# A hand-written order of the last ten tiles is replaced, the last tile's sums go to two PSUM banks, and one copy of queries moves ahead of a transpose

## The chip, the cores and the metric

The kernel runs on one core of one Trainium2 chip. The metric is device time in microseconds of one execution. The engines are TensorE (PE; its weight loads are listed apart as PEld), VectorE (DVE), ScalarE (ACT), GpSimd (POOL) and SyncE (SP), which only issues transfers here. Each engine works through its own instructions in the order in which the program gives them; between engines there are semaphores. PE writes to PSUM, which has eight banks of 128 partitions by 512 fp32 numbers.

## The reference

Cross-attention with a residual and a layer norm. `x` has 4 batches of 2048 rows of 512, the context 4 times 77 rows, and there are 16 heads of 32:

```python
qs = (q @ wq).reshape(Bq, Lq, H, HD).transpose(0, 2, 1, 3)
ks_ = (k @ wk).reshape(Bq, Lk, H, HD).transpose(0, 2, 1, 3)
vs = (v @ wv).reshape(Bq, Lk, H, HD).transpose(0, 2, 1, 3)
scores = jnp.einsum('bhqd,bhkd->bhqk', qs, ks_) / jnp.sqrt(jnp.float32(HD))
scores = jnp.where(mask[:, None, :, :], -jnp.inf, scores)
attn_w = jax.nn.softmax(scores, axis=-1)
attn = jnp.einsum('bhqk,bhkd->bhqd', attn_w, vs)
attn = attn.transpose(0, 2, 1, 3).reshape(Bq, Lq, H * HD)
out = attn @ wo + q
mu = jnp.mean(out, axis=-1, keepdims=True)
var = jnp.mean((out - mu) ** 2, axis=-1, keepdims=True)
return (out - mu) / jnp.sqrt(var + EPS) * gamma + beta
```

Here `q` is `x` and `k` and `v` are the context.

## The kernel before

The 8192 rows are 64 tiles of 128 rows. Tiles t = 2b and 2b + 1 make pair b; four tiles make a group, whose queries come from one block of transposed `x`. Products in full precision are made of three fp32r matmuls each (a number is split into a high and a low part). The first three pairs are written out in a loop of their own; pairs 3 to 26 run the list of words `PAIR`; what is left of the last pairs and tiles 54 to 63 is the list `JOINT` and then `ORDER`, which `do()` carries out word by word. The words set the order in which each engine gets its instructions, and nothing else does. A word is a letter, a tile (or pair, or query block) and a part; in `PAIR` the number is relative to the pair.

- `S54` scores of tile 54 (PE, L321), four banks, one for each fourth of the heads. `T54.1` the maxima of one fourth, 4 heads (DVE, L364), which reads the second of these banks and adds the mask. `e54.1` the exponentials (ACT, L379), `r54` the reciprocals of the sums (DVE, L385), `n54` the normalising product (POOL, L390), `t54` a transpose in blocks of 32 (DVE, L413).
- `P26.7g` the seventh of twelve transfers that regroup the transposed pair 26 into `PT` (L425); the last letter names the queue that issues it: s is SP, a is ACT, g is POOL. `U62.7s` is the same for tile 62 alone. `V26` then multiplies pair 26 with the values (PE, L459; two banks, half of the heads to each), `a26.0` and `b26.0` split the first half's result into high (ACT, L508) and low (DVE, L512).
- `O54` the output projection of tile 54 (PE, L557; one bank, 12 matmuls), `x54` loads its rows, `+54` adds them (DVE, L560).
- `Q59` queries of block 59, that is a fourth of the columns for one group (PE, L192; one bank), `q59` copies them out (DVE, L209). `i31` and `j31` split half a group of transposed `x` (ACT, POOL).
- Layer norm: `s` mean and variance on DVE (L595, L601), or `I` and `J` the same on ACT (L615, L621); `u` the reciprocal root on POOL (L631, L632); then either `y` and `z` on DVE (L655, L664), or `v`, `k` and `f` on POOL, ACT and POOL (`p` is `v` and `k` in one on POOL, L645), or `y`, `K` and `G` on DVE, ACT and POOL. `w` stores the tile.
- Tile 63 has a way of its own: `h`, `m`, `R` and `E` turn it with PE, `W` multiplies one tile with the values (L492, L474), `c` and `d` split it, `X63` adds its rows by matmuls with the identity (L540), and `O63` goes by halves of the columns. `finish_last` stores by halves, on SP and ACT.
- `M0` and `M1` keep the rows gamma and beta in a PSUM bank from there on, which leaves the ring one bank fewer.

`bank()` (L107) deals the eight banks in turn: a tile gets the buffer of the eighth grant before it, and its first matmul waits until that buffer's last reader is through. The order of the grants is that of the words.

The words on PE in `ORDER` run: S54 O49 S55 Q59 O48 S56 V25 S57 Q62 Q60 Q63 S58 Q61 V26 S59 O51 O50 S60 V27 S61 O52 O53 O54 S62 V28 O55 O57 S63 V29 O56 O59 O58 V30 R63.0 R63.1 R63.3 R63.2 O60 O61 X63 W62 W63 O62 O63.

For tile 54 the word `y54` (which subtracts the mean in place and multiplies by gamma) stands ahead of `J54` (which sums the squares about the mean).

## Time and profile before

| | us |
|---|---|
| three runs | 507.15, 506.95, 507.97; median 507.15 |
| the profiled execution | 506.96 |
| its span, first to last instruction | 505.2 |
| outside its span | 1.76 |
| PE, granted clock over the span | 0.998 |
| ORDER on PE, first to last matmul | 413.48 to about 498.6 |

The profile's times count from the first instruction. The page gives the busy time of each engine, the chain of waits that ended last, and groups of equal instructions; the trace behind it gives rows in order of time (start, length, engine, line, operation, tiles), busy times by stretch, and a list of who waited for whom. A row's length can overlap the next one's on the same engine, so what an instruction costs in a full queue is the distance from its start to the next start.

### The profile page before, as it was taken

Reading aid. Unit: us, or ns where it says so; the run is one execution under the profiler, and the core shown is the slowest. Engines: PE = TensorE matmul, PEld = TensorE weight load, DVE = VectorE, ACT = ScalarE, POOL = GpSimd, SP = SyncE. Lnnn points to the kernel's source line nnn. Section 1 sums busy time; section 2 is a strip of 40 time slices with the busy share of each in tenths; the row PEclk is TensorE's granted clock in tenths of the full one; section 3 lists DMA queues with packets and bytes.
Section 4 is the critical chain, followed back from the end, with each engine's and each line's share of the span. In section 5 each row is a group of like instructions: output and inputs, shape, how many; then the busy total and the mean of one; then the engine's idle time right before and its main releaser. Section 6 shows DMA issues by size and latency. Waiting matters only on the chain.

```text
span 505.2 us, 20438 instructions
## 1 busy us (share of the span) xinstructions
PE 496.4 (98%) x6908; PEld 391.0 (77%) x6908; DVE 463.3 (92%) x2566; ACT 472.2 (93%) x2239; POOL 427.0 (85%) x384
## 2 busy tenths in 40 slices
PE   9999999999999999999999999999999999999994
PEld 7987778777777887777788777777877777777784
DVE  6698999999989998999999988999999889999997
ACT  6798999999999999999999999999999999999861
POOL 0659368989888998988999888889988888999994
PEclk9999999999999999999999999999999999999999
DMA  8945887677778779777878878787777878667665
GB/s 308 399 165 151 207 215 194 197 191 210 213 226 227 217 211 257 188 205 227 224 218 220 237 182 248 210 228 212 228 200 204 237 214 245 171 189 209 168 210 209
DMA packets 58280, 109.50 MB, mean 217 GB/s; under 512 B 9203, under 2 KB 10739, under 8 KB 58176
## 3 DMA queue, kind: packets, MB, share of 16 engines
q1 hardware_dynamic: 55776, 103.35, 72.5%
q0 software_dynamic: 1872, 4.20, 2.7%
q8 instruction: 55, 0.90, 0.8%
q10 hardware_dynamic: 528, 0.66, 0.4%
q14 instruction: 49, 0.40, 0.2%
HBM read 41.68 MB, written 16.78 MB: 116 GB/s over the span
## 4 chain that ended last, share of the span: by engine, by line
PE 90%; ACT 4%; DVE 3%; DMA 2%; issue 1%; SPq 1%; DVEq 0%; ACTq 0%
PE pq L192 31%; PE po L557 29%; PE pa L459 11%; PE sc L321 7%; PE sc L557 3%; ACT pbuf L379 3%; PE sc_e L321 2%; PE pv L258 2%; PE pk L218 1%; PE pq L709 1%; PE pq L190 1%; DMA PT<-B 1%; PE sc_f L321 1%; DMA xtf<-xT 1%; DVE pbuf L364 1%
## 5 line engine op out<-in xcount | busy, mean ns | idle before, releaser
L379 ACT ACTIVATE pbuf<-pbuf,nm 128x77 f32<-128x77 f32 x1024 | 352.5, 349 | 8.5 <-DVE nm L364 7.5
L379 ACT ACTIVATION_READ_ACCUMULATOR pbuf<-pbuf,nm 128x1 f32 x1024 | 193.5, 189 | 0.0
L390 POOL TENSOR_TENSOR pbuf<-pbuf,ri 128x1232 f32<-128x1232 f32 x63 | 145.9, 2317 | 19.7 <-DVE ri L385 15.7
L364 DVE CUSTOM_DVE_ANT_0 pbuf<-sc,mb 128x77 f32<-128x77 f32 x828 | 144.0, 232 | 5.9 <-PE sc L321 5.6
L192 PE MATMUL pq<-xtl,wqh 128*128 128x512 f32 (+1 forms) x256 | 98.3, 384 | 0.0
L192 PE MATMUL pq<-xth,wql 128*128 128x512 f32 (+1 forms) x256 | 98.2, 384 | 0.0
L413 DVE STREAM_TRANSPOSE B<-pbuf 128x1280 f32<-128x1280 f32 x63 | 94.6, 1503 | 0.4 <-POOL pbuf L390 0.2
L557 PE MATMUL po<-woh,AH 128*128 128x512 f32 x224 | 90.6, 405 | 0.0
L192 PE MATMUL pq<-xth,wqh 128*128 128x512 f32 (+1 forms) x230 | 88.6, 385 | 0.0
L557 PE MATMUL po<-wol,AH 128*128 128x512 f32 x224 | 87.4, 390 | 0.0
L585 POOL TENSOR_TENSOR o<-o,gam 128x512 f32<-128x512 f32 x53 | 68.7, 1297 | 21.0 <-ACT o L581 21.0
L557 PE MATMUL po<-woh,AL 128*128 128x512 f32 x224 | 86.5, 390 | 0.0
L364 DVE DVE_READ_ACCUMULATOR2_ANT nm<- 128x1 f32 x1024 | 84.7, 83 | 0.0
L586 POOL TENSOR_TENSOR o<-o,bet 128x512 f32<-128x512 f32 x53 | 68.4, 1290 | 4.2
L180 POOL TENSOR_TENSOR xtl<-xtf,xth 128x1024 fp32r<-128x1024 f32 x28 | 67.5, 2412 | 0.1
L459 PE MATMUL pa<-PT,vsb 96*32 96x256 f32 x960 | 58.2, 382 | 0.7 <-DMA PT<-B 0.3
L321 PE MATMUL sc<-kct,q 32*64 32x77 f32 x3312 | 55.2, 238 | 0.5 <-DVE q L209 0.5
L192 PEld LDWEIGHTS pq<-xth,wql 128*128 128x128 f32 x256 | 48.2, 188 | 8.4
L192 PEld LDWEIGHTS pq<-xtl,wqh 128*128 128x128 f32 x256 | 48.1, 188 | 8.5
L321 PEld LDWEIGHTS sc<-kct,q 32*64 32x64 f32 x3312 | 48.7, 130 | 6.5 <-issue 4.8
L557 PEld LDWEIGHTS po<-woh,AH 128*128 128x128 f32 x224 | 42.0, 188 | 10.8 <-DVE nm L364 0.4
L192 PEld LDWEIGHTS pq<-xth,wqh 128*128 128x128 f32 x230 | 43.2, 188 | 9.0
(176 smaller groups left out, 851.6 us busy)
## 6 DMA issues: line engine op xcount, KB each, us to landing
PT<-B SPq DMA_DIRECT2D x355, 128.0 KB
xtf<-xT SPq DMA_DIRECT2D x28, 512.0 KB
o<-x SPq DMA_DIRECT2D x56, 256.0 KB
out<-o SPq DMA_DIRECT2D x56, 256.0 KB
PT<-B POOLq DMA_DIRECT2D x16, 128.0 KB, 4.5
o_end<-x SPq DMA_DIRECT2D x7, 256.0 KB
out<-o_end SPq DMA_DIRECT2D x7, 256.0 KB
xtf<-xT SPq DMA_DIRECT2D x4, 256.0 KB
```

The source lines that it names most:

```text
L180: nc.gpsimd.tensor_tensor(l, fx.pop((g, c)), h.bitcast(F32), ALU.subtract)
L192: nc.tensor.matmul(pq, wc, r[:, c, rs], start=(n == 0), stop=(n == 11))
L258: nc.tensor.matmul(pv, ctx_s[c][i][:, r, :], v[c], start=(n == 0), stop=(n == 11))
L321: nc.tensor.matmul(scs[t][g, j][r0 : r0 + n], qd[t // 4][q, g, at : at + n], kct[q, g, t // TPB, keys_of(j)], start=True, stop=True,)
L364: nc.vector.tensor_tensor_reduce(pb[:, i // 2, (i % 2) * NK : (i % 2 + 1) * NK], scs[t][g, j], mb[:, t % TPB, keys_of(h)], -1.0, CEIL, ALU ...
L379: nc.scalar.activation(p, p, AF.Exp, bias=nmax[t][:, i : i + 1], scale=-1.0, accum_out=sums[t][:, i : i + 1])
L390: nc.gpsimd.tensor_tensor(pv, pv, rv.to_broadcast((P, NP, 2, NK)), ALU.mult)
L413: nc.vector.transpose(bt.rearrange("p c q r -> p q c r"), pbuf[t % NPB].rearrange("p q (c r) -> p q c r", c=5),)
L459: nc.tensor.matmul(pas[b, g // 2][HD * j : HD * (j + 1), (g % 2) * BLK : (g % 2 + 1) * BLK], vsb[:, 2 * b // TPB, HD * h : HD * (h + 1)], ...
L557: nc.tensor.matmul(pos[t][:, cols], a[:, c, rs], w[:, c, cols], start=go, stop=done)
L585: nc.gpsimd.tensor_tensor(o, o, gam, ALU.mult)
L586: nc.gpsimd.tensor_tensor(o, o, bet, ALU.add)
```

## The change

- `JOINT` and `ORDER` are replaced by one new list. Nearly all words are the same ones in another order. Gone are I54 and J54, s58, s60, s62, v56, k56, f56 and p50; new are s54 (ahead of y54), I58, J58, I60, J60, I62, J62, y56, K56, G56, v50 and k50. The transfers change queues: on POOL's there are 15 for 16, on ACT's 5 for 3, the rest is on SP's.
- The words on PE now run: S54 Q59 S55 S56 O48 O49 S57 V25 Q63 S58 Q62 Q61 Q60 S59 V26 S60 O51 O50 S61 V27 O52 O53 S62 V28 O54 O55 O57 S63 V29 O56 O58 O59 V30 R63.1 R63.0 O61 R63.3 R63.2 O60 W62 W63 O62 X63 O63.
- The words on DVE now begin: q58 b24.0 T54.1 T54.0 T54.3 T54.2 b24.1 q59 T55.2 T55.3 T55.0 t53 T56.2 T56.1 r54 T56.3 +48 T55.1 T56.0 s48 t54 T57.3; around tile 59 they run q60 T59.0 q62 T59.2 T59.1 T59.3 t57, around tile 62 t59 T62.2 b27.0 +52 T62.1; and they end with z61 z58 +62 d63 y60 z60 y62 s63 z62 y63 z63.
- M0 comes later, and M1 is the last word but one, behind z63, so that beta is read from SBUF.
- Tile 63's projection has a PSUM bank for each half of the columns, and `X63`, the statistics and `y63` go by these halves.
- In pair 3 the word q6 (the copy of query block 12) is put ahead of t0; before, that copy was the first DVE work of pair 4's q4.

```diff
-JOINT = """ a24.1 b24.0 b24.1 """
-
 ORDER = """
-S54 T54.3 i31 e54.3 T54.0 O49 q58 e54.0 k47 T54.2 T54.1 +49 t53 S55 T55.0 T55.1 Q59 f47 x50 x52 T55.3 e54.2 T55.2
-e54.1 j31 r54 n54 O48 q59 s49 P26.9s +48 S56 e55.0 P26.4s e55.2 e55.1 e55.3 T56.1 T56.0 P26.6g P26.0s V25 T56.2 x51
...
+q58 i31 b24.0 S54 T54.1 k47 Q59 T54.0 a24.1 T54.3 e54.1 T54.2 b24.1 e54.2 S55 q59 j31 S56 T55.2 e54.0 T55.3 T55.0 O48
+e54.3 t53 f47 x61 e55.0 T56.2 P26.3s T56.1 P26.5s e55.2 r54 T56.3 n54 P26.0s +48 w47 e55.3 T55.1 O49 x58 T56.0 S57
+P26.11s P26.6g e55.1 s48 V25 x50 t54 u48 x52 e56.1 x51 P26.1g T57.3 x59 Q63 P26.4g e56.3 r55 P26.9s T57.0 n55 T57.2
+P26.2s e56.0 T57.1 P26.8s +49 P26.10s S58 p48 e56.2 t55 x53 Q62 a25.0 T58.0 P27.9s e57.3 P26.7g r56 b25.0 x57 n56
+T58.3 P27.2s a25.1 Q61 s49 e57.2 P27.10s b25.1 P27.5s T58.2 P27.0g e57.0 x56 q63 P27.1g x55 Q60 f48 q61 e57.1 P27.4s
+t56 P27.6s k46 P27.11s T58.1 e58.3 P27.7s r57 S59 q60 n57 P27.3s T59.0 e58.1 P27.8s q62 V26 T59.2 e58.2 f46 T59.1 S60
+T59.3 a26.1 O51 t57 a26.0 e58.0 T60.1 P28.8s P28.5g T60.0 e59.3 P28.9g w46 O50 T60.2 u49 P28.6s T60.3 e59.1 P28.10g
+P28.1s r58 +51 P28.3g P28.2s b26.0 n58 e59.0 b26.1 S61 x54 +50 e59.2 V27 P28.4s s51 P28.11s s50 u51 e60.0 P28.7s r59
+t58 O52 n59 a27.1 e60.1 T61.0 T61.2 P28.0g e61.2 T61.1 O53 p49 b27.1 T61.3 a27.0 e61.3 t59 u50 S62 e61.1 v51 T62.2
+P29.10s P29.7g b27.0 V28 P29.5s f49 e61.0 +52 x62 T62.1 P29.3s O54 a28.0 +53 a28.1 P29.6s r61 s52 e60.3 n61 P29.1s s53
...
+O63 w58 I62 y60 w61 J62 z60 y62 w60 u62 s63 w59 z62 u63 y63 w62 z63 M1 w63
@@ resid
-        pos[t] = bank(f"po_{t}")
-        if t < NT - 4:
-            nc.tensor.matmul(pos[t], ident, od[t], start=True, stop=False)
-            return
+        pos[t] = [bank(f"po_{t}")[:, cols] for cols in HALVES]
         place(t)
...
-                nc.tensor.matmul(pos[t][:, c * P : (c + 1) * P], rows_t, unit, start=(c == 0 and n == 0), stop=False)
+                po = pos[t][c // 2][:, c % 2 * P : (c % 2 + 1) * P]
+                nc.tensor.matmul(po, rows_t, unit, start=(c % 2 == 0 and n == 0), stop=False)
@@ o_proj
-        halves = [slice(0, D)] if t < NT - 1 else HALVES
-        for cols in halves:
+        for po, cols in [(pos[t], slice(0, D))] if first else zip(pos[t], HALVES):
             for n, (_, c, a, w) in enumerate(prods):
...
-                nc.tensor.matmul(pos[t][:, cols], a[:, c, rs], w[:, c, cols], start=go, stop=done)
+                nc.tensor.matmul(po, a[:, c, rs], w[:, c, cols], start=(first and n == 0), stop=(n == 11))
@@ moments_one
-            for n, cols in enumerate(HALVES):
-                nc.vector.bn_stats(st[:, n], pos.get(t, od[t])[:, cols])
+            for n, po in enumerate(pos[t]):
+                nc.vector.bn_stats(st[:, n], po)
@@ centre
+        for po, cols in zip(pos[t], HALVES):
+            nc.vector.scalar_tensor_tensor(od[t][:, cols], po, mean, gam[:, cols], ALU.subtract, ALU.mult)
@@ pair
             words.insert(words.index("D"), "O-6")
+            words.insert(words.index("t0"), "q6")
```

More of the change, by code (lines that the diff above doesn't have):

```diff
@@ L51 @@
 """
-JOINT = """ a24.1 b24.0 b24.1 """
 ORDER = """
-S54 T54.3 i31 e54.3 T54.0 O49 q58 e54.0 k47 T54.2 T54.1 +49 t53 S55 T55.0 T55.1 Q59 f47 x50 x52 T55.3 e54.2 T55.2
-e54.1 j31 r54 n54 O48 q59 s49 P26.9s +48 S56 e55.0 P26.4s e55.2 e55.1 e55.3 T56.1 T56.0 P26.6g P26.0s V25 T56.2 x51
-r55 a25.0 a25.1 t54 e56.1 S57 e56.2 T56.3 T57.2 Q62 P26.2g P26.8s n55 e56.3 T57.1 Q60 t55 u49 b25.0 e56.0 P26.3g Q63
-e57.1 p49 e57.2 T57.3 T57.0 r56 w47 s48 b25.1 P26.5s x59 e57.3 x53 S58 P26.10s P26.7g P27.7g q62 e57.0 k46 n56 q60
@@ L59 @@
-P27.0s q63 u48 p48 T58.1 T58.2 P26.1s P27.1s P26.11s T58.3 e58.1 r57 t56 P27.11s n57 Q61 P27.6s f46 e58.2 T58.0 V26
-q61 a26.1 t57 a26.0 x55 f48 e58.0 S59 P27.2s T59.2 P27.5s e58.3 T59.3 e59.3 P27.3s P28.4g P27.8s T59.0 O51 b26.0
-P28.11g T59.1 P27.9s +51 P28.6g r58 e59.2 P28.5g O50 P27.10s b26.1 s51 e59.1 P27.4s n58 S60 Y0 u51 +50 P28.0s x57
-e59.0 P28.7g P28.10s V27 T60.0 T60.1 a27.0 T60.2 a27.1 T60.3 e60.1 r59 t58 w46 P28.3s P28.9s S61 n59 O52 P28.1s
-e60.3 b27.0 s50 T61.0 T61.3 t59 f49 u50 e61.0 e61.3 T61.2 b27.1 T61.1 O53 P28.8s P29.1g P29.9g e61.2 O54 S62 +52
@@ L64 @@
-e61.1 +53 s52 x54 r61 P28.2s V28 +54 P29.7g e60.2 x62 T62.1 T62.2 O55 p50 n61 e60.0 T62.3 x56 P29.4s r60 n60 T62.0
-t61 v51 M0 P29.8s a28.0 a28.1 b28.1 b28.0 f50 t60 +55 O57 e62.2 P29.6s e62.1 P29.5s P29.10s +57 P30.6g P29.3s
-P29.11s k51 P29.2s P29.0s P30.10s P30.1s e62.0 e62.3 u52 v52 S63 V29 P30.2s T63.0 P30.9s P30.5g s53 P30.7g P30.11a
-s55 T63.1 r62 a29.1 P30.4s T63.3 P30.0s e63.0 P30.3s n62 b29.1 T63.2 O56 a29.0 b29.0 e63.1 I54 u53 e63.3 P30.8s s57
-h63.0 y55 t62 +56 f51 O59 u55 e63.2 x58 O58 x60 k52 m63.0 y54 V30 h63.1 m63.1 I56 U62.7s U62.6s +59 J56 a30.1 u56
@@ L69 @@
-U62.4s U62.8s R63.0 U62.9s x61 U62.11s s59 y57 a30.0 u57 +58 u59 b30.1 b30.0 U62.5s z57 R63.1 y53 J54 R63.3 U62.1s
-U62.0a R63.2 w48 E63.0a f52 w51 s58 U62.10s O60 U62.3s +60 w50 O61 U62.2a w52 y58 X63 M1 z53 E63.1a v56 v59 s60 z55
-+61 y60 E63.2a u54 W62 u58 k56 E63.3a w49 w57 u60 z54 k59 c62 w54 I61 J61 W63 f56 z58 c63 d62 y61 w53 z60 w55 u61
-f59 O62 w56 d63 z61 +62 s62 y62 w58 w61 w59 O63 u62 s63 z62 w60 y63 u63 w62 z63 w63
+q58 i31 b24.0 S54 T54.1 k47 Q59 T54.0 a24.1 T54.3 e54.1 T54.2 b24.1 e54.2 S55 q59 j31 S56 T55.2 e54.0 T55.3 T55.0 O48
@@ new lines @@
+T59.3 a26.1 O51 t57 a26.0 e58.0 T60.1 P28.8s P28.5g T60.0 e59.3 P28.9g w46 O50 T60.2 u49 P28.6s T60.3 e59.1 P28.10g
+P28.1s r58 +51 P28.3g P28.2s b26.0 n58 e59.0 b26.1 S61 x54 +50 e59.2 V27 P28.4s s51 P28.11s s50 u51 e60.0 P28.7s r59
+t58 O52 n59 a27.1 e60.1 T61.0 T61.2 P28.0g e61.2 T61.1 O53 p49 b27.1 T61.3 a27.0 e61.3 t59 u50 S62 e61.1 v51 T62.2
+P29.10s P29.7g b27.0 V28 P29.5s f49 e61.0 +52 x62 T62.1 P29.3s O54 a28.0 +53 a28.1 P29.6s r61 s52 e60.3 n61 P29.1s s53
+x60 e60.2 T62.0 P29.0s O55 T62.3 P29.4s u53 b28.1 P29.11a k51 P29.2s r60 t61 n60 e62.0 P29.8s P29.9s b28.0 O57 e62.3
@@ new lines @@
++54 f51 t60 e62.2 S63 +57 P30.0s e62.1 y53 V29 P30.5s u52 T63.0 P30.6s +55 P30.9a v50 P30.3g P30.10s r62 O56 s55 a29.1
+v52 P30.11s P30.2a s54 n62 a29.0 P30.7s k50 b29.0 P30.1s e63.0 T63.1 P30.8s b29.1 O58 f50 t62 P30.4s e63.1 T63.3
+U62.11s O59 M0 h63.0 e63.3 U62.4s T63.2 m63.0 U62.8s y54 U62.0s +58 e63.2 U62.7g w50 U62.1g Y0 V30 +59 u55 k52 s57 u54
+U62.9s a30.0 +56 U62.10s u57 R63.1 h63.1 R63.0 a30.1 y55 U62.2s m63.1 I56 b30.0 w49 b30.1 O61 U62.3s J56 z54 U62.6a
+u56 E63.1a z55 U62.5a R63.3 f52 y57 R63.2 w55 E63.3a O60 +61 I58 w48 s59 w51 E63.0a E63.2a w54 z53 I61 u59 y56 w53 J58
@@ L73 @@
+W62 +60 J61 u58 z57 W63 c62 y61 w57 u61 K56 y58 v59 I60 d62 O62 G56 J60 z61 z58 k59 u60 w56 X63 c63 +62 w52 f59 d63
+O63 w58 I62 y60 w61 J62 z60 y62 w60 u62 s63 w59 z62 u63 y63 w62 z63 M1 w63
 """
@@ L551, in o_proj @@
             prods.sort(key=lambda p: p[0])
-        halves = [slice(0, D)] if t < NT - 1 else HALVES
-        for cols in halves:
+        for po, cols in [(pos[t], slice(0, D))] if first else zip(pos[t], HALVES):
             for n, (_, c, a, w) in enumerate(prods):
-                go = first and n == 0 and cols.start == 0
-                done = n == 11 and cols.stop == D
-                nc.tensor.matmul(pos[t][:, cols], a[:, c, rs], w[:, c, cols], start=go, stop=done)
+                nc.tensor.matmul(po, a[:, c, rs], w[:, c, cols], start=(first and n == 0), stop=(n == 11))
     def residual(t):
@@ L653, in centre @@
     def centre(t):
-        row = gam if t in pos else rows.get(0, gam)
-        nc.vector.scalar_tensor_tensor(od[t], pos.pop(t, od[t]), mvs[t, 1][:, 0:1], row, ALU.subtract, ALU.mult)
+        mean = mvs[t, 1][:, 0:1]
+        if t < NT - 1:
+            nc.vector.scalar_tensor_tensor(od[t], od[t], mean, rows.get(0, gam), ALU.subtract, ALU.mult)
+            return
+        for po, cols in zip(pos[t], HALVES):
+            nc.vector.scalar_tensor_tensor(od[t][:, cols], po, mean, gam[:, cols], ALU.subtract, ALU.mult)
     def finish_last(t):
@@ L953, in xattn_layernorm @@
         pair(n)
-    for word in (JOINT + ORDER).split():
+    for word in ORDER.split():
         do(*read(word))
```

## The prediction

> **What bounds the kernel now.** First the page's head: the span and the busy shares. Then the busy time of the engines by stretch over the part that the change rewrites, and last what TensorE (PE) waited for.

> ```profile
> span 505.2 us, 20438 instructions
> PE 496.4 (98%) x6908; PEld 391.0 (77%) x6908; DVE 463.3 (92%) x2566; ACT 472.2 (93%) x2239; POOL 427.0 (85%) x384
> ```
> ```profile
> 425.00:440.00 15.00, 15.00 (x214) 11.61 (x213) 14.53 (x101) 15.00 (x82) 14.40 (x15) 1.00 0.73 204
> 440.00:455.00 15.00, 14.92 (x293) 11.18 (x293) 14.93 (x90) 15.00 (x81) 14.73 (x14) 1.00 0.73 192
> 455.00:470.00 15.00, 14.71 (x207) 11.36 (x207) 14.81 (x79) 15.00 (x80) 14.32 (x15) 1.00 0.63 172
> 495.00:505.20 10.20, 3.61 (x28) 3.29 (x26) 6.99 (x14) 0.00 (x0) 4.08 (x7) 0.92 0.58 221
> ```
> ```profile
> PE sc L321 <- DVE q L209: 0.5, 1, 0.5
> PE pa L459 <- DMA PT<-B: 0.3, 1, 0.3
> PE pa L459 <- issue: 0.2, 1, 0.2
> ```

> The stretches give window and length, then busy PE, PEld, DVE, ACT, POOL, granted clock, DMA share, GB/s. From the start of ORDER on PE (413.48, below) to its last matmul (about 498.6) PE works without a hole but for the last two waits, 0.54 us in all. PE is the bound, and it has nothing in reserve: whatever newly holds PE there is added to the time. VectorE (DVE) is nearly as full, so it has no lead by which it could hand over PSUM banks sooner.

> **Prices.** PE, then DVE, in the first microseconds of ORDER. The pitch is from start to start.

> ```profile
> 413.48 0.95 PE L321 MATMUL sc<-kct,q 32*64 32x77 f32 x64
> ...
> 417.29 0.95 PE L321 MATMUL sc<-kct,q 32*64 32x77 f32 x64
> 418.17 0.50 PE L192 MATMUL pq<-xth,wqh 128*128 128x512 f32 x1
> ...
> 421.03 0.39 PE L557 MATMUL po<-woh,AH 128*128 128x512 f32 x1
> ...
> 423.84 0.95 PE L321 MATMUL sc<-kct,q 32*64 32x77 f32 x64
> ...
> 424.87 1.93 PE L459 MATMUL pa<-PT,vsb 96*32 96x256 f32 x32
> ...
> 426.74 0.95 PE L321 MATMUL sc<-kct,q 32*64 32x77 f32 x64
> ```
> ```profile
> 414.23 0.69 DVE L512 TENSOR_TENSOR AL<-pa,AH 128x512 fp32r<-128x512 f32 x1 [0.17 <-ACT AH L508]
> ...
> 414.84 0.23 DVE L364 CUSTOM_DVE_ANT_0 pbuf<-sc,mb 128x77 f32<-128x77 f32 x1
> ```
> ```profile
> 418.57 1.50 DVE L413 STREAM_TRANSPOSE B<-pbuf 128x1280 f32<-128x1280 f32 x1
> 419.99 0.20 DVE L364 CUSTOM_DVE_ANT_0 pbuf<-sc,mb 128x77 f32<-128x77 f32 x1
> ...
> 422.50 0.25 DVE L385 RECIPROCAL ri<-sum 128x16 f32<-128x16 f32 x1
> 422.66 0.63 DVE L209 COPY q<-pq 128x512 f32<-128x512 f32 x1
> 423.21 0.68 DVE L595 BATCH_NORM_STATS2 st<-o 128x6 f32<-128x512 f32 x1
> ...
> 424.02 0.67 DVE L560 TENSOR_TENSOR o<-po,o 128x512 f32<-128x512 f32 x1
> ```

> PE: S 0.88, Q and O 2.86 behind S (2.81 behind each other), V 1.87. DVE: t 1.42; the 16 heads of a tile 422.50 − 419.99 = 2.51, so a quarter T 0.63; r 0.16, q 0.55, s 0.81, b (and +, of the same shape) 0.61.

> **The change: banks.** `bank()` deals eight PSUM banks in turn, in the order of the words: S takes four, V two, Q and O one. A word thus gets the bank of the eighth grant before it, and its matmuls wait until that one's last reader is through. In ORDER before, these waits are over in time, or PE would show holes. In the new order I counted the grants and added up DVE's words between the release of one thing and the next. Each sum starts from an event DVE itself must wait for, so DVE cannot be early:

> 1. S55 takes the banks of Q58, V24 (both) and S54's first; the last one free is V24's, by b24.1, which now stands behind all of T54. S54 is out at 414.43 (413.48 + 0.95); T54 2.51 and b 0.61 make 417.55. PE is there after Q59: 413.48 + 0.88 + 2.86 = 417.22. **0.35** lost.
> 2. O48 takes S55's first bank. Behind S55's end DVE does T55.2, T55.3, T55.0: 1.89. PE has only S56, 0.88, in between. **1.0**.
> 3. O49 takes S55's second bank, read by T55.1, which stands behind t53, T56.2, T56.1, r54, T56.3, +48. From T55.0's end: 1.42 + 1.26 + 0.16 + 0.63 + 0.61 + 0.63 = 4.71; PE has O48, 2.86. **1.85**. S57 then needs T56.0, 0.63 later: hidden under O49.
> 4. V26's second bank is Q62's; q62 stands behind T59.0. From S59's end 0.63 + 0.55 = 1.18, against half a V, 0.93: 0.25. S60 then needs T59.1: 1.26 against the other half, 0.93: 0.33. Together **0.6**.
> 5. V28 follows S62 directly and takes V27's first bank, freed by b27.0 behind T62.2. From S62's end 0.63 + 0.61 = **1.25**.

> Sum 5.05; a handover from PE to DVE and back costs a little each time (S59 of the trace starts 0.25 after its bank is free, but PE was busy until then, so 0 to 0.25). I take 0.03 for each of the six, 5.2. ACT's a24.1, which now stands behind i31 and k47, must be out by 416.9 for place 1; if it isn't, that place grows.

> With these waits PE's starts, by the pitches above, are: O49 425.2, S57 428.1, V25 428.9, Q63 430.8, S58 433.7, Q62 434.5, Q61 437.4, Q60 440.2, S59 443.0, V26 443.9, S60 446.4, O51 447.3, O50 450.2, S61 453.0, V27 453.9, O52 455.8, O53 458.6, S62 461.5, V28 463.7.

> **Transfers.** The page's group of n on POOL, and its list of issues (last figure: issue to landing).

> ```profile
> L390 POOL TENSOR_TENSOR pbuf<-pbuf,ri 128x1232 f32<-128x1232 f32 x63 | 145.9, 2317 | 19.7 <-DVE ri L385 15.7
> ```
> ```profile
> PT<-B POOLq DMA_DIRECT2D x16, 128.0 KB, 4.5
> ```

> The pieces of P28 go out late, and V28 is now before O54. The last, P28.0g on POOL, stands behind n59, which needs r59; that comes on DVE behind +50, s51 and s50, after O50 is out at 453.0: 0.61 + 0.81 + 0.81 + 0.16 make 455.4; n59 2.3 makes 457.7, and 4.5 to landing 462.2. V28 has its bank at 463.7: hidden, with 1.5 in hand, and the old waits of 0.3 and 0.2, at V28 and behind S63, go: **−0.54**. P29, P30 and U62 have over 2 us by the same count, as PE is late by then; without that cover a late one costs what the 0.3 row shows. SP's queue loses nothing in order: x61 first on it only reuses a buffer free long before. The pieces on POOL's queue go from 16 to 15, and to ACT's from 3 to 5 at no busy time.

> **Query copy of pair 3.**

> ```profile
> 75.15 0.63 DVE L209 COPY q<-pq 128x512 f32<-128x512 f32 x1
> ...
> 75.83 0.97 PE L321 MATMUL sc<-kct,q 32*64 32x77 f32 x66 [0.46 <-DVE q L209]
> ```
> ```profile
> 118.63 0.21 DVE L385 RECIPROCAL ri<-sum 128x16 f32<-128x16 f32 x1
> 118.76 0.63 DVE L209 COPY q<-pq 128x512 f32<-128x512 f32 x1
> ```
> ```profile
> 119.40 0.28 PE L321 MATMUL sc_e<-kct,q 32*64 32x77 f32 x1
> ```

> The copy waits behind a reciprocal, which waits for ACT's exponentials; moved ahead, up to 0.46 goes. But three pairs on the same copy ends at 119.39 and the scores start at 119.40: a PE that came 0.46 early would wait there for ACT's chain. Between 0 and 0.46; I take **−0.2**.

> **Statistics and the tail.** s58, s60, s62 (0.81 each) leave DVE for I and J on ACT, which is idle in the last 10 us (the 0.00 above); I54 and J54 go, s54 comes to DVE; tile 56 gains a y on DVE in place of k on ACT, and POOL gets one G for its f; p50 leaves POOL for v50 and ACT's k50. All of it lies ahead of a PE that is now late: 0, and about 1 us if PE were not. M0 and M1 come later, so banks stay in the ring longer: in the count above already. Tile 63's tail:

> ```profile
> 497.97 0.64 PE L557 MATMUL pa<-woh,AL 128*128 128x256 f32 x4
> ```
> ```profile
> 498.32 0.75 DVE L655 SCALAR_TENSOR_TENSOR o_end<-o_end,mvt,row 128x512 f32<-128x512 f32 x1
> 498.99 0.76 DVE L599 BATCH_NORM_STATS2 small<-pa 128x6 f32<-128x256 f32 x2
> 499.77 0.21 DVE L601 BATCH_NORM_AGGREGATE mvt<-small 128x2 f32<-128x12 f32 x1
> 499.90 0.69 DVE L664 SCALAR_TENSOR_TENSOR o_end<-o_end,mvt,pa 128x512 f32<-128x512 f32 x1
> 500.51 0.74 DVE L655 SCALAR_TENSOR_TENSOR o_end<-pa,mvt,gam 128x512 f32<-128x512 f32 x1
> 501.36 0.87 DVE L660 SCALAR_TENSOR_TENSOR o_end<-o_end,mvt,pa 128x256 f32<-128x256 f32 x2
> ```

> Before: 498.61 to 502.23, 3.62. After: y62 is out of the way and the first half's statistics, in a bank of their own, run under the second half's matmuls; left are 0.4 for the second half, 0.2, z62 0.6, y63 in two halves 0.87 (as the two of L660), z63 0.87: 2.95. **−0.65**. POOL's u63 runs beside z62 and y63: from the statistics' end to its own it took 0.9.

> ```profile
> 500.06 0.19 POOL L631 TENSOR_TENSOR mvt<-mvt,small 128x1 f32<-128x1 f32 x1 [0.88 <-DVE mvt L601]
> 500.33 0.55 POOL L632 TENSOR_TENSOR mvt<-mvt,small 128x1 f32<-128x1 f32 x1
> ```

> **The sum**, against the profiled execution, 506.96 with 1.76 outside its span (0.19 below the median of the three): +5.2 − 0.54 − 0.2 − 0.65 = +3.8, **510.8 us**. Ends: with no handovers and 0.46 for the copy 510.4; if places 1 and 4 clear because DVE came sooner, 509.4; with 0.25 a handover and nothing for the copy 512.3. Own range 509.4 to 512.3.

> **Rivals.**
> - *Faster: PE does not wait at the new bank reuses.* Mechanism at O48 and O49: the old bank counts as free sooner, or PE takes S57 first. The point is whether O49 can start before T55.1 has ended. Then 5.2 falls out: 506.96 − 0.54 − 0.2 − 0.65 = 505.6. For it speaks that no hole of this kind is in the trace; against it that the old order never asked for one. [...] Chance 0.11.
> - *Partly: only places 2, 3 and half of 5 hold,* because DVE catches up in what s58 to s62 left. 506.96 + 3.5 − 1.4 = 509.1, just at the edge; with place 5 gone too 508.4. Chance 0.10.
> - *Slower still.* Late PE makes ACT late: a28 waits for V28, the exponentials of tiles 60 and 62 stand behind it, and t60, P30 and V30 follow; up to 1.5. Or PE's clock falls in the holes: in the last stretch it is 0.92 over 10.2 us, as if halved for 1.6 us, that is 5 us after the last matmul; the holes at O48 and O49 make 2.85 in 5.7 us. Were it halved there for as long, 5 us of matmuls would take 2.5 more: 513.3. [...] Chance 0.12 for 512.3 to 514.
> - That the transfers still decide (V28 waiting for its pieces again) is inside the forecast's range: 0.3 beside a bank wait of 1.25.

> **How the numbers follow.** Forecast 0.67, the others 0.11, 0.10, 0.12. A measurement of this kernel tells 0.2%, 1.0 us, from no change. Faster 0.11; same 0.04 (the low end of the partial case); slower 0.85. The range 507.8 to 513.2 holds the forecast, most of the partial case and half of the slower one, about 8 in 10.

> **What would show it.** Right: in PE's waits new rows for L557, L459 and L321 behind DVE's L364, L512 and L209; O49 (the second group of 12 at L557 in ORDER) starts at T55.1's end near 425, three late; a hole of over 1 us between the scores of tile 62 and the next L459; the last matmul near 503. Wrong: a PE as dense as before from 413 on, or that hole filled. The copy's step: no wait at 75.8, and the scores near 119 no more than 0.46 earlier. The tail: 3.0 from the last matmul to the last DVE instruction.

## The result, and the profile after

The changed kernel took 512.29 us (median of seven executions, 509.33 to 514.45) beside 507.31 us of the kernel before: a ratio of 1.0088, 95% interval 1.0059 to 1.0116. It is slower, by about 5 us where 3.8 was forecast. A second set of five executions gave 509.54 beside 507.26, 1.0045 (1.0032 to 1.0058). The forecast of 510.8 lies between the two. The way there was another one, though. (One execution of a variant below, the one with its loads put late, ran at a mean clock of 0.685 and took 845.82; its median leaves that one out.)

The profiled execution is the slowest of the seven, 514.45. Its head and clock row:

```profile
span 512.7 us, 20444 instructions
PE 501.8 (98%) x6908; PEld 394.5 (77%) x6908; DVE 469.4 (92%) x2564; ACT 477.8 (93%) x2248; POOL 426.7 (83%) x381
...
PEclk9999999999999999999999999999999999889999
```

The span is cut in three: up to the start of V24, from there to the last matmul's end, and what follows. The middle part, by the view of stretches (window, length, busy PE, PEld, DVE, ACT, POOL, clock, DMA share, GB/s), before, after, and in the second set's profiled execution:

```profile
411.61:498.61 87.00, 86.31 (x1220) 67.17 (x1219) 83.33 (x419) 76.85 (x366) 80.09 (x90) 1.00 0.71 202
```
```profile
411.76:506.16 94.40, 91.02 (x1220) 69.97 (x1219) 86.02 (x416) 80.97 (x374) 79.36 (x87) 0.96 0.70 186
```
```profile
411.78:501.78 90.00, 87.86 (x1220) 67.69 (x1219) 84.84 (x417) 80.43 (x374) 79.41 (x86) 1.00 0.73 195
```

V24 starts 0.15 later than before, and DVE ends 3.63 behind the last matmul where it was 3.62; so the span's 7.5 us all lie in the middle part: +7.40. PE's idle time there grew from 0.69 to 3.38. Its busy time grew by 4.71 for the same 1220 matmuls, and most of that is the clock, which is 0.96 on the mean. In the second set's execution the clock stays at 1.00 and the part takes 90.00, three more than before.

Where the long execution lost its time: the chain of waits, and then DVE's row and PE's rows at that place (the bracket is the idle time ahead of the row and what ended it).

```profile
428.69 8.53 DMA PT<-B
437.23 4.38 DMA PT<-B
441.63 1.51 DVE B L411
```
```profile
441.63 1.51 DVE L411 STREAM_TRANSPOSE B<-pbuf 128x1280 f32<-128x1280 f32 x1 [2.62 <-DMA PT<-B]
```
```profile
441.81 1.07 PE L457 MATMUL pa<-PT,vsb 96*32 96x256 f32 x16 [0.18 <-DMA PT<-B]
443.81 1.07 PE L457 MATMUL pa<-PT,vsb 96*32 96x256 f32 x16 [0.93 <-DVE nm L362]
...
445.75 0.37 PE L319 MATMUL sc<-kct,q 32*64 32x77 f32 x2 [0.20 <-DVE q L207]
446.47 1.36 PE L319 MATMUL sc<-kct,q 32*64 32x77 f32 x58 [0.35 <-DVE nm L362]
...
497.45 1.08 PE L490 MATMUL sc<-PT,vsb 96*32 96x128 f32 x32 [0.81 <-DMA PT<-B]
```

The transpose t56 overwrites the buffer from which the pieces of P26 are being read, so it waits until they have landed: 2.62 us, with DVE doing nothing. T58.1, q60, q62 and the maxima T59 stand behind t56 on DVE, and V26's second half and S60 wait for them on PE (the rows at 443.81, 445.75 and 446.47). The pieces are late because the new order sets row loads (x, 256 KB each) among them on SP's queue, as two runs below show. From issue to landing, in the view of the tile `PT` over 418 to 445, before and after:

```profile
DMA to landing us min/median/max: 2.3/3.9/4.9
```
```profile
DMA to landing us min/median/max: 5.3/7.2/8.2
```

Then the clock falls. Two half-microsecond stretches of the long execution:

```profile
445.50:446.00 0.50, 0.30 (x3) 0.19 (x2) 0.50 (x6) 0.50 (x3) 0.50 (x1) 0.94 0.94 147
452.50:453.00 0.50, 0.50 (x3) 0.36 (x3) 0.00 (x0) 0.50 (x5) 0.48 (x2) 0.74 1.06 303
```

Between them every stretch is at 0.50. A mean of 0.94 is half clock for the last 0.06 us, 0.74 for the first 0.26, so PE ran at half clock from 445.94 to 452.76, 6.82 us. Half of that, 3.4, is the estimate of its cost; O51's matmuls start 0.43 apart in it, but for the first, and those of O50 0.23 apart behind it, which would make 3.1. The 3.4 is three quarters of the distance between this execution (94.40) and the second set's (90.00).

### The profile page after: what moved, and what is told of

It reads as the page before. It is cut to its first block, busy times and chain, and to the rows that moved or that the text cites. A ratio compares the mean times of both kernels' runs of the same rounds, so it can differ in the third digit from the quotient of the medians.

```text
span 512.7 us, 20444 instructions
## 1 busy us (share of the span) xinstructions
PE 501.8 (98%) x6908; PEld 394.5 (77%) x6908; DVE 469.4 (92%) x2564; ACT 477.8 (93%) x2248; POOL 426.7 (83%) x381
## 4 chain that ended last, share of the span: by engine, by line
PE 90%; DVE 5%; DMA 3%; SPq 1%; issue 0%; POOL 0%; POOLq 0%; ACT 0%; DVEq 0%; ACTq 0%
PE po L550 33%; PE pq L190 30%; PE pa L457 10%; PE sc L319 8%; DMA PT<-B 3%; PE sc_e L319 2%; PE pv L256 2%; PE pk L216 1%; PE pq L706 1%; PE pq L188 1%; PE sc_f L319 1%; DVE o_end L661 1%; DVE o_end L649 1%; PE pw L673 1%; SPq L527 1%; DVE o_end L553 1%
## 5 line engine op out<-in xcount | busy, mean ns | idle before, releaser
L377 ACT ACTIVATE pbuf<-pbuf,nm 128x77 f32<-128x77 f32 x1024 | 354.8, 349 | 11.0 <-DVE nm L362 10.2
L388 POOL TENSOR_TENSOR pbuf<-pbuf,ri 128x1232 f32<-128x1232 f32 x63 | 146.0, 2317 | 24.7 <-DVE ri L383 16.8
L550 PE MATMUL po<-woh,AH 128*128 128x512 f32 (+1 forms) x252 | 101.7, 405 | 0.0
L550 PE MATMUL po<-wol,AH 128*128 128x512 f32 (+1 forms) x252 | 98.2, 391 | 0.0
L550 PE MATMUL po<-woh,AL 128*128 128x512 f32 (+1 forms) x252 | 93.9, 390 | 0.0
L362 DVE DVE_READ_ACCUMULATOR2_ANT nm<- 128x1 f32 x1024 | 82.4, 80 | 0.1
L319 PE MATMUL sc<-kct,q 32*64 32x77 f32 x3328 | 57.5, 240 | 0.9 <-DVE nm L362 0.6
L550 PEld LDWEIGHTS po<-woh,AH 128*128 128x128 f32 x252 | 47.9, 190 | 12.6 <-issue 0.6
L319 PEld LDWEIGHTS sc<-kct,q 32*64 32x64 f32 x3328 | 50.3, 131 | 7.1 <-issue 4.6
L550 PEld LDWEIGHTS po<-woh,AL 128*128 128x128 f32 x252 | 47.4, 190 | 10.2
L550 PEld LDWEIGHTS po<-wol,AH 128*128 128x128 f32 x252 | 47.9, 190 | 8.8
## 6 DMA issues: line engine op xcount, KB each, us to landing
PT<-B SPq DMA_DIRECT2D x356, 128.0 KB
PT<-B POOLq DMA_DIRECT2D x13, 128.0 KB, 4.3
```

Source lines behind the costliest of these rows:

```text
L319: nc.tensor.matmul(scs[t][g, j][r0 : r0 + n], qd[t // 4][q, g, at : at + n], kct[q, g, t // TPB, keys_of(j)], start=True, stop=True,)
L362: nc.vector.tensor_tensor_reduce(pb[:, i // 2, (i % 2) * NK : (i % 2 + 1) * NK], scs[t][g, j], mb[:, t % TPB, keys_of(h)], -1.0, CEIL, ALU ...
L377: nc.scalar.activation(p, p, AF.Exp, bias=nmax[t][:, i : i + 1], scale=-1.0, accum_out=sums[t][:, i : i + 1])
L388: nc.gpsimd.tensor_tensor(pv, pv, rv.to_broadcast((P, NP, 2, NK)), ALU.mult)
L550: nc.tensor.matmul(po, a[:, c, rs], w[:, c, cols], start=(first and n == 0), stop=(n == 11))
```

## Experiments

Theory A: the row loads set among P26's pieces make those late, t56 waits for them, and the rest follows. Theory B, the prediction's own kind: the order of the words and the reuse of banks hold PE, whatever the transfers do. Theory C: the holes drop the granted clock, and that is the larger part and the scatter. Theory D: the tail wins nothing because z reads beta from SBUF beside POOL.

Each run was timed in five rounds beside the kernel before. "The stretch" is PE from V24's start to its last matmul's end in the profiled execution.

### Once more

> The changed kernel once more, beside its variants on one chip. Theory A (late transfers): t56 waits 0.9 to 2.6 us for its DMAs in the profiled execution, and the median is 511 to 512.5 with a spread of 3 us or more. Rival: the first seven executions were high by chance; the median is 509 to 510, as that of the variants so far.

Measured: 509.54 (508.96 to 510.28); in the profiled execution t56 waits 1.09 us, and there is no half clock. Theory A was right on the wait and wrong on the median and the spread; the rival was right on the median. The same program thus waited 1.1 us at t56 in one execution and 2.6 in the other, and the medians of its two sets lose 2.3 us and 5. The mean granted clock of each execution shows part of the difference: in the first set it is 0.992 to 0.994 in three of the seven (514.45, 512.93 and 512.29 us) and 0.996 or more in the others, in the second 0.996 or more in all five. In 75 executions of the kernel before it is never under 0.995. It is not the whole scatter, since one execution of the first set took 512.48 at 0.996.

### Loads early in the kernel before

Order on SP's queue (P are pieces, x row loads, w row stores):

```diff
- x50 x52 P26.9 P26.4 P26.0 x51 P26.8 w47 P26.5 x59 x53 P26.10
+ x61 P26.9 x58 P26.4 x50 P26.0 x52 x51 P26.8 x57 w47 P26.5 x56 x59 x53 P26.10
```

> The kernel before with six row loads moved in SP's queue: x56, x57, x58 and x61 forward to stand among the pieces of P26, and x50 and x52 back to the same place. No other word moves. Theory A (late transfers): t56 waits for DMAs for 1 to 2.6 us, PE gets holes behind it near 440, the granted clock may halve there, and the time is 509 to 513, against 507.3. Theory B: no wait at t56 that PE feels, the time within 1 us of 507.3.

Measured: 508.76, ratio 1.0031 (1.0010 to 1.0052). The stretch is 87.50 instead of 87.00, and DVE shows the wait that the kernel before does not have:

```profile
440.73 1.51 DVE L413 STREAM_TRANSPOSE B<-pbuf 128x1280 f32<-128x1280 f32 x1 [1.01 <-DMA PT<-B]
```

So the bunching makes the wait by itself, with no other word moved (the pieces land in 6.8 us at the median instead of 3.9), and it costs about 1.4 us at the median. Theory A was right on the wait and gave 509 to 513 for the time, a little too much; theory B gave less than 1 us. Three of the twelve executions (510.29, 511.03 and 511.29 us) have a mean clock of 0.993.

### Loads late, or spread, in the changed kernel

```diff
- x61 P26.3 P26.5 P26.0 w47 x58 P26.11 x50 x52 x51 x59 P26.9 ... P27.9 x57 P27.2 P27.10 P27.5 x56 x55
+ P26.3 P26.5 P26.0 w47 P26.11 x50 x52 x51 x59 P26.9 ... P28.2 x57 x54 ... P29.8 x56 ... P30.8 x58 ... U62.11 x61
```

> The changed kernel with the row loads of x56, x57, x58 and x61 taken from among the pieces of P26 and P27 and put back behind P28, P29, P30 and U62. Theory A (late transfers): the last pieces of P26 land before DVE reaches t56, its wait of 2.6 us in the changed kernel is under 0.5, the granted clock stays 1.00 from 440 to 455, and the time is 507 to 509, against 512.3 of the changed kernel. Theory B (the order of the words and the reuse of banks hold PE, the transfers are beside the point): the time stays within 1 us of 512.3, and the holes at V26 stay.

Measured: 509.61, ratio 1.0049 (1.0028 to 1.0069), the stretch 90.06. t56 no longer waits and the clock holds, as theory A had it; yet the time is above its 507 to 509, and the stretch is as long as the second set's. V29 waits for its pieces in place of t56; x56 now stands ahead of the last of them:

```profile
472.21 1.93 PE L457 MATMUL pa<-PT,vsb 96*32 96x256 f32 x32 [1.42 <-DMA PT<-B]
```

Next the loads went to stretches with few transfers: x50 and x52 ahead of P26, x59, x57 and x61 behind P27, and x62, x60, x58 and x56 in one go behind P28.7.

> The changed kernel with its row loads spread over stretches in which few transfers run: x50 and x52 ahead of the pieces of P26 (as the kernel before has them), x57, x59 and x61 behind P27, x62, x60, x58 and x56 behind P28. Theory A (late transfers): no DMA wait over 0.3 at t56 or ahead of any V, PE from V24's start to its last matmul 88.0 to 88.7 (87.0 before, 94.4 in the changed kernel, 90.1 with the loads put late), the time 508.0 to 508.8. Theory B (the order of the words and banks): small waits inside S and O for DVE stay and hold that stretch at 89.5 or more, the time 509.5 or more.

Measured: 511.15, ratio 1.0078 (1.0060 to 1.0096), the stretch 93.60. There was a new hole at V28, and a half clock after it:

```profile
461.32 3.25 PE L457 MATMUL pa<-PT,vsb 96*32 96x256 f32 x32 [2.20 <-DVE AL L510]
```

The row names DVE, whose b27 was long done. By the landings, it waited for a piece. SP issued the four loads at 453.8 to 456.3, and pieces of that time took 4.2 to 6.9 us to land, where the second set's execution had 2.4 to 4.5. The last piece of pair 28, P28.0g, was issued at 454.81 and landed 5.9 us later; V28 starts 0.6 behind that. In the next run, spread2, the same piece was issued at 455.68 and took 4.3, and V28 starts 0.5 behind its landing, which fits the same wait. That run took the four loads apart (x60 alone behind P28.7, the others among P30):

> The changed kernel with its row loads spread, this time without the four behind P28 that stood in the way of P28.0g in the run spread: x50 and x52 ahead of P26, x59 and x57 behind P27, x61 behind w46, x60 alone behind P28.7, x58, x56 and x62 among the pieces of P30. Theory A (late transfers): without the 2.2 us hole and the half clock of spread, whose stretch on PE from V24's start to the last matmul was 93.6, there is left 93.6 - 2.2 - 3.4 = 88.0; no half clock, time 507.7 to 508.7, against 509.5 of the changed kernel on the last chip and 507.3 of the kernel before. Theory B: 89.5 or more on PE, 509.3 or more.

Measured: 509.99, ratio 1.0061 (1.0035 to 1.0088), the stretch 89.58 with the clock at 1.00. The transfers of 418 to 445 land in 4.0 us at the median, as before the change, and t56 does not wait. Theory A gave 88.0 and fell; the stretch lies in theory B's range of 89.5 or more.

What is left is seen by taking the time between the starts of successive V's on PE. Rows of the kernel before, then of the second set's execution, then of spread2:

```profile
439.95 1.93 PE L459 MATMUL pa<-PT,vsb 96*32 96x256 f32 x32
...
449.39 1.93 PE L459 MATMUL pa<-PT,vsb 96*32 96x256 f32 x32
...
461.78 1.93 PE L459 MATMUL pa<-PT,vsb 96*32 96x256 f32 x32 [0.29 <-DMA PT<-B]
```
```profile
426.00 1.93 PE L457 MATMUL pa<-PT,vsb 96*32 96x256 f32 x32
...
441.84 1.93 PE L457 MATMUL pa<-PT,vsb 96*32 96x256 f32 x32 [0.18 <-DVE nm L362]
...
452.49 1.93 PE L457 MATMUL pa<-PT,vsb 96*32 96x256 f32 x32
```
```profile
426.00 1.93 PE L457 MATMUL pa<-PT,vsb 96*32 96x256 f32 x32
...
441.84 1.93 PE L457 MATMUL pa<-PT,vsb 96*32 96x256 f32 x32 [0.18 <-DMA PT<-B]
...
451.44 1.93 PE L457 MATMUL pa<-PT,vsb 96*32 96x256 f32 x32 [0.18 <-DMA out<-o]
```

From each distance the words between are taken off at the prediction's prices (S 0.88, Q and O 2.86 behind S or V and 2.81 behind each other, V 1.87), which leaves what PE lost there, in us:

| from, to | before | after, long | after, second set | spread2 |
|---|---|---|---|---|
| V24, V25 | 0.22 | 0.31 | 0.30 | 0.31 |
| V25, V26 | 0.11 | 0.85 | 0.87 | 0.87 |
| V26, V27 | 0.14 | 5.85 | 1.35 | 0.30 |
| V27, V28 | 0.28 | 0.40 | 0.37 | 0.65 |
| V28, V29 | 0.30 | 0.04 | 0.54 | 0.07 |
| V29, V30 | -0.09 | -0.10 | -0.10 | 0.51 |
| sum | 0.96 | 7.35 | 3.33 | 2.71 |

From V30 to the last matmul it is the same work in all: 17.85 before, 18.86, 18.48 and 18.68 after. The late transfers are the line V26 to V27, and spreading the loads brings it to 0.30. Against the second set, spread2 gains 1.52 in this line and V28 to V29, and V27 to V28 and V29 to V30 take 0.89 of it back. The line V25 to V26 is the same with any placing of the loads (late_loads too has 15.82 between these V's). It comes from S58. PE and DVE in spread2 at that place:

```profile
430.84 0.36 PE L319 MATMUL sc<-kct,q 32*64 32x77 f32 x6
431.45 0.90 PE L319 MATMUL sc<-kct,q 32*64 32x77 f32 x58 [0.25 <-DVE nm L362]
```
```profile
431.16 0.23 DVE L362 CUSTOM_DVE_ANT_0 pbuf<-sc,mb 128x77 f32<-128x77 f32 x1
...
431.31 0.69 DVE L553 TENSOR_TENSOR o<-po,o 128x512 f32<-128x512 f32 x1
```

S58 has the four banks free only when T57's last maximum is read, at 431.39. In the new order it stands behind S57, V25 and Q63; before there were three Q's between. This is a bank wait of the kind that the prediction was looking for, in a place it had not named. The other two lines in which spread2 loses clearly more than the kernel before hold waits for transfers again: at V28 for P28.0g, as above, and ahead of V30 0.52, where the row names a transfer. So theory B's range was met, but of its reason, banks and order whatever the transfers do, the trace shows only S58's line, 0.76 more than before.

### A filled hole

The first sixteen matmuls of V26 done twice:

```diff
-        for g in range(NG):
+        for g in (0, 1, 0, 1, 2, 3) if b == 26 else range(NG):
```

> The changed kernel with the first sixteen matmuls of V26 done twice (the same values to the same place), 0.93 us of work in the 0.93 us in which PE waits between V26's halves. Theory C (the granted clock falls because of PE's idle time near 441 to 446): the clock stays 1.00 from 445 to 453 or is halved for less than half of the 6.8 us, the time is 509 to 510 although t56 waits for its transfers as before, and the executions differ by less than 2 us, against 5 of the changed kernel. Rival: the holes that are left (0.2, 0.2, 0.35 us) and PE's thin work there do it alone: the clock halves as before, time within 1 us of 512.3.

Measured: 510.30, executions from 509.68 to 511.71, the clock at 1.00 from 440 to 455. That is what theory C gave, but it decides little: t56 waited only 0.90 us here, and the second set's execution waited 1.09 and kept its clock with no filler. None of the eleven executions has a mean clock under 0.995, but neither has any of the second set's five. Inconclusive.

### The banks

A pool of eight tiles, each with a name of its own, taken strictly in turn:

```diff
-        ring.append(ring[-8] if kept else ps.tile([P, 512], F32, tag="mm", name=name))
+        own = not kept and ps.tile([P, 512], F32, tag=f"mm{len(ring) % 8}", bufs=1, name=name)
+        ring.append(ring[-8] if kept else own)
```

> The changed kernel with the eight PSUM banks dealt strictly in turn, as the prediction took them to be. If the prediction's sums for its five places were right under that rule: holes of 0.3 ahead of S55, about 1.0 ahead of O48, 1.8 ahead of O49, 0.6 at V26 and S60, 1.2 ahead of V28, 3.5 to 5 us of new idle time on PE, and 2 to 5 us more time than the changed kernel's on the same chip (some comes back, since P26 lands in time for a later t56). Rival: DVE catches up and the rule is worth less than 1 us either way.

Measured: 518.78 beside 509.54 of the changed kernel on the same chip. The profiled execution is the slowest of six, 523.54, with a half clock. V24 starts at 415.93, 4.1 late, so the rule costs in the tiles ahead too. Behind that, PE's rows that waited:

```profile
422.15 1.68 PE L320 MATMUL sc<-kct,q 32*64 32x77 f32 x124 [0.15 <-DVE AL L511]
425.26 0.47 PE L551 MATMUL po<-woh,AH 128*128 128x512 f32 x1 [1.44 <-ACT pbuf L378]
...
430.16 0.47 PE L551 MATMUL po<-woh,AH 128*128 128x512 f32 x1 [1.90 <-DVE nm L363]
...
454.46 0.90 PE L320 MATMUL sc<-kct,q 32*64 32x77 f32 x33 [1.86 <-issue]
...
474.43 1.93 PE L458 MATMUL pa<-PT,vsb 96*32 96x256 f32 x32 [1.47 <-DVE AL L511]
```

These are S55 (0.15, forecast 0.35), O48 (1.44, forecast 1.0), O49 (1.90, forecast 1.85), S60 (1.86, forecast 0.33) and V28 (1.47, forecast 1.25). O48's row names ACT, so its size agrees only by and large; at S60 the place was right and the size far off. The sums were good, by and large, for the rule they were made with. The kernel does not follow that rule.

> The kernel before with the eight PSUM banks dealt strictly in turn. In ring_after the last ten tiles began 4.1 us late (V24 at 415.9 instead of 411.8) and then took 98.9 instead of 90.0 from V24 to the last matmul. If the order before, unlike the changed one, fits that rule (as the prediction had it, for lack of holes in its trace): V24 near 415.9, then 87 to 88.5, time 511 to 513. If the pool's choice served that order too: V24 to the last matmul 90 or more, time 514 or more.

Measured: 513.17, between the two forecasts; V24 at 414.75 and the stretch 91.69 in the profiled execution, the slowest of five (515.03). The order before does not fit the rule either, for a hole of 2.78 at S60, with a half clock behind it:

```profile
457.81 0.58 PE L322 MATMUL sc<-kct,q 32*64 32x77 f32 x31 [2.78 <-issue]
```

### The tail

M1, the copy of beta into PSUM, put ahead of E63.1a:

```diff
- ... u56 E63.1a z55 ... u63 y63 w62 z63 M1 w63
+ ... u56 M1 E63.1a z55 ... u63 y63 w62 z63 w63
```

> The changed kernel with M1, ACT's copy of beta into a PSUM bank, moved from behind z63 to the place ahead of E63.1a, so that every z but z54 reads beta from PSUM. Theory D (z with beta in SBUF is held up by POOL's use of SBUF at the same time): the z rows that took 1.5 to 1.6 us (z53, z58 or z61, z60) come back to 0.74, the end of DVE behind the last matmul shrinks from 3.6 to about 3.0, and the time is 0.5 to 0.8 below the changed kernel's. Rival: DVE is held up by what is queued ahead of it anyway, z rows shorten but the end behind the last matmul stays at 3.4 or more and the time within 0.3.

Measured: 509.40, ratio 1.0038 (1.0017 to 1.0060), which can't be told from 1.0045; a gain in time is not shown. In the profiled execution the z's are back at 0.69 to 0.75 each, but for z54 (1.00), which stands ahead of M1, and DVE ends 2.89 behind the last matmul, which ended at 501.54:

```profile
502.17 0.69 DVE L661 SCALAR_TENSOR_TENSOR o_end<-o_end,mvt,po 128x512 f32<-128x512 f32 x1
502.78 0.48 DVE L652 SCALAR_TENSOR_TENSOR o_end<-po,mvt,gam 128x256 f32<-128x256 f32 x1
503.18 0.48 DVE L652 SCALAR_TENSOR_TENSOR o_end<-sc,mvt,gam 128x256 f32<-128x256 f32 x1
503.57 0.86 DVE L657 SCALAR_TENSOR_TENSOR o_end<-o_end,mvt,po 128x256 f32<-128x256 f32 x2
```

The tail alone in the kernel before: two banks for tile 63, and X63 behind O62 instead of ahead of M1.

> The kernel before with the changed kernel's two banks for tile 63's halves, its residual matmuls X63 moved to stand between O62 and O63, and nothing else. The prediction's tail step (y62 out of the way, the first half's statistics under the second half's matmuls, 3.62 to 2.95) by itself: O62, +62, s62 and y62 come 1 us earlier against the last matmul, PE's dense stretch stays 87.0, DVE ends 2.9 behind the last matmul; time 506.4 to 507.0, against 507.3. Rival: DVE's work ahead of it (z61, d63) holds y62 back, the end stays at 3.3 or more, the time within 0.3.

Measured: 507.14, ratio 0.9992 (0.9983 to 1.0002). The distance from the last matmul to DVE's end fell to 2.97, but by the last matmul's coming 0.40 later (499.01); DVE's end moved only from 502.23 to 501.98. DVE has no idle time from 494 on, so what is ahead of y62 on it (d63, z61, +62, s62) sets the end. That is the rival's reason and its time, though not its distance of 3.3 or more. No run here is faster than the kernel before by more than the measurement can tell.

### All mends together

> Three mends in one: the row loads spread as in the run spread, M1 ahead of E63.1a as in beta_early, and the two pieces of U62 that were on ACT's queue put on SP's, ahead of Y0 and of the row stores w50 and w49. If A and D hold and W62's wait for its pieces (0.8 to 1.3 us) goes: the end of DVE 2.9 behind the last matmul, no wait at W62, time 506.3 to 507.5, the kernel before (507.3) or up to 1 us under it. If theory B holds the order itself costs 2 us or more: 508.5 or more.

Measured: 510.08, ratio 1.0061 (1.0046 to 1.0076): no wait at W62 and the tail short, but it kept spread's hole at V28 (2.21) and its half clock.

> spread2 with M1 ahead of E63.1a and U62's two pieces from ACT's queue on SP's, ahead of Y0, w50 and w49. The end of DVE 2.9 behind the last matmul instead of 3.6, no wait at W62: 0.7 to 1 us below spread2, 506.7 to 507.8 if A holds, so between the kernel before and 0.6 us under it. Theory B: 508.6 or more.

Measured: 509.76, ratio 1.0057 (1.0038 to 1.0075). The wait moved on once more: with Y0 put behind the pieces, W63 waits 0.99 for what Y0 loads, and V30 0.63 for transfers:

```profile
482.33 1.93 PE L457 MATMUL sc<-PT,vsb 96*32 96x256 f32 x32 [0.63 <-DMA o_end<-x]
...
493.87 0.27 PE L472 MATMUL pa<-PT,spare 77*32 77x128 f32 x1 [0.99 <-DMA spare<-vsb]
```

The stretch is 90.26. The time is in theory B's range of 508.6 or more, but these two waits are for transfers.

## Why the prediction was right in its number and wrong in its reason

The number was luck. The largest term of the sum, 5.2 for the banks, did not come about as reckoned. In its place came a wait for transfers that the sum had at nothing, smaller bank waits in other places and, in some executions, the half clock of a rival; and the gains of 0.54, 0.2 and 0.65 did not come.

**What bounds the kernel: right.** PE has nothing in reserve; its new holes are in the time, and mending one (t56's, the tail's, W62's) gave little or nothing while the next stood. Only at the very end of the order before, DVE sets the time: in before_tail's profiled execution the last matmul came 0.40 later and DVE's end 0.25 earlier.

**Banks, the step that failed.** "`bank()` deals eight PSUM banks in turn", and so does the section on the kernel. It does so only from M0 on, where the ring of the last eight is used again. Until then it asks a pool of eight tiles of one name, and in the program as built the new tile gets the free bank whose last reader stands earliest in the words. All grants from S54 to M0 go that way, in both kernels; 55 of the 68 after the change, and 34 of the 58 before it, are not the eighth grant before. O48 thus gets S55's third bank, not its first, and needs T55.2 alone. PE and DVE of the changed kernel, long execution, at the place where 1.0 and 1.85 were forecast:

```profile
417.48 1.88 PE L319 MATMUL sc<-kct,q 32*64 32x77 f32 x128
419.32 0.47 PE L550 MATMUL po<-woh,AH 128*128 128x512 f32 x1
...
424.94 0.95 PE L319 MATMUL sc<-kct,q 32*64 32x77 f32 x64
```
```profile
420.36 1.51 DVE L411 STREAM_TRANSPOSE B<-pbuf 128x1280 f32<-128x1280 f32 x1
```

O48 starts at 419.32, right behind S56 (S55 and S56 are the x128) and a microsecond before T55.0 ends (t53, right behind it, starts at 420.36); O48 and O49 take 5.62 together, with no hole. At V26 the prediction had the second half wait for q62. That half did wait, 0.93 us, but for T58.1, and it starts at 443.81, before q62:

```profile
445.01 0.68 DVE L207 COPY q<-pq 128x512 f32<-128x512 f32 x1
```

That there were no holes in the trace of before was taken as a sign that its order fits the rule; ring_before, with its 2.78, shows that the trace could not say so. DVE's own work had been summed well, as ring_after shows at four of the five places.

**Transfers: failed, in the place that decided.** "SP's queue loses nothing in order" looked at x61 alone, and at when P28 lands, not at the row loads set among P26's pieces. Their landing went from 3.9 to 7.2 us, and t56 waited 1.1 to 2.6. The -0.54 forecast became a loss of 1.2 to 5.7 (V26 to V27 against before, the half clock included). The two old waits of 0.3 did not go either: V28 waited 0.3 in both executions, and V29 0.5 in the second set's. W62, which had "over 2 us" in hand, waited 0.8 in the long execution.

**Clock: the rival came about.** It had 0.12 and a price of 2.5; the long execution paid 3.4 by the estimate above. What the prediction had of the clock was one fall in the trace of before, at 503.60, 5.0 us after the last matmul's end (the mean over 503.50 to 504.00 is 0.60, behind that 0.50). Here it fell with no hole over 0.93 in the preceding 4 us.

**Query copy: no gain.** Its wait of 0.5 near 75.8 is gone, but V24 starts at 411.76 against 411.61, and at 410.99 to 412.88 in the nine profiled runs of the new order without the ring. Of the 0 to 0.46 it was the 0, within that scatter.

**Tail: -0.65 forecast, 0 measured.** The order of steps was right (2.89 in beta_early, 2.95 forecast), but what was overlooked is M1. With beta still in SBUF, z reads o or o_end and bet from there (the rows below), and so does POOL's product beside it. DVE and POOL in the long execution:

```profile
494.74 1.59 DVE L661 SCALAR_TENSOR_TENSOR o<-o,mvt,bet 128x512 f32<-128x512 f32 x1
...
504.48 1.53 DVE L661 SCALAR_TENSOR_TENSOR o_end<-o_end,mvt,bet 128x512 f32<-128x512 f32 x1
505.94 0.73 DVE L649 SCALAR_TENSOR_TENSOR o_end<-o_end,mvt,row 128x512 f32<-128x512 f32 x1
```
```profile
504.18 1.29 POOL L579 TENSOR_TENSOR o_end<-o_end,bet 128x512 f32<-128x512 f32 x1
```

z60 begins 0.30 behind POOL's product and ends 0.54 behind that product's end: it took 1.53 instead of 0.74. z53, and one of z61 and z58, go the same way. In beta_early the z's with beta in PSUM took 0.69 to 0.75. In the second set's execution z53 and z60 began first, at 490.73 and 500.32, and took 0.72 and 0.75. There POOL's products, 0.03 and 0.15 later, took 1.84 and 1.75 in place of 1.29:

```profile
500.47 1.75 POOL L579 TENSOR_TENSOR o_end<-o_end,bet 128x512 f32<-128x512 f32 x1
```

So in these pairs the one that began second took longer than its usual 0.74 or 1.29. Whether the two hold each other up in SBUF, as theory D has it, was not shown beyond these times. In the second set's execution DVE still ended 3.67 behind the last matmul, since z62 had to wait 0.48 for POOL:

```profile
503.13 0.75 DVE L661 SCALAR_TENSOR_TENSOR o_end<-o_end,mvt,bet 128x512 f32<-128x512 f32 x1 [0.48 <-POOL mvt L625]
```

**What stays open.** With t56's wait gone and the clock whole, the new order still costs 2 to 3 us (stretches of 89.58 and 90.26 against 87.00), in waits of 0.2 to 1.0 at S58, V28, V30 and in the last 18 us. S58's was traced to its bank and V28's to P28.0g; the loss of 0.6 to 1.0 behind V30 is W62's or W63's wait only in part. No order of the loads that frees all of these at once was found, so how much of the cost is the order of the words alone is not shown. How often an execution falls to half clock is told only by the mean clocks given above, as only one of each set has a profile.

## What to carry to other kernels

How buffers are handed out is an input of such a sum: read it from the program as built, or find one row that only the assumed rule explains, since a trace without waits fits many rules. A row load may hold nothing up by its place in its queue's order and still lengthen the landing of the pieces beside it, here from 3.9 to 7.2 us, so look at the transfers of the few microseconds ahead of whoever waits for them. Where one engine has no reserve, compare a fixed stretch of it with the sum of its own prices, part by part; mending the largest wait then shows what the next one gives back.

## What the runs showed of the hardware

```profile
458.00:458.50 0.50, 0.50 (x32) 0.35 (x23) 0.19 (x2) 0.37 (x3) 0.50 (x2) 0.65 0.56 172
461.50:462.00 0.50, 0.50 (x4) 0.42 (x3) 0.50 (x5) 0.50 (x4) 0.18 (x2) 0.94 1.01 369
```

That is from 458.15 to 461.56. The longer ones are twice that. What sets these lengths no run shows. The longest hole ahead of one of these falls was 2.78 us, in ring_before; in the long execution it was 0.93, and the clock fell 2.1 us behind its end. The length of one hole did not decide: in ring_after the clock fell at 453.78, 1.2 us into the hole of 1.86 at S60, while 1.90 between O48 and O49 in the same execution did not lower it, nor did 1.42 in late_loads. All five falls stood at V and S words, whose rows have tile sizes of 96*32 and 32*64 where those of Q and O have 128*128; whether that is the cause was not tried.
